# Counting negative entries on GpSimd and TensorE, and a scratch tile for ScalarE's passes, in a two-layer graph kernel

## The chip, the cores and the metric

The kernel runs on one core of a Trainium2 chip. The metric is device time in microseconds (us), the median of three runs.

## The reference

The inputs are `x` (2708 x 512), a sparse non-negative adjacency matrix `adj` (2708 x 2708) and small weights, all float32. Two layers are computed:

```
rowsum = adj.sum(axis=1);  d = where(rowsum > 0, rowsum ** -0.5, 0)
x = layernorm(x + relu((d[:, None] * adj * d[None, :]) @ x @ W + b))
# layer 1: mean over 4 heads of softmax(logits + NEG * (1 - adj)) @ feats, then relu
x = layernorm(x + layer_1(x, adj, W_node, b_node, K))
```

With `NEG` = -1e10, the softmax of a row picks the row's largest entry. The kernel uses that each row of `adj` holds only a few entries. It is exact only where no entry is negative and some other conditions hold, so it keeps a tile `bad` of alarms. If any alarm is set at the end, a dense version (`dense_layers`) runs instead. With the inputs given it does not run.

## The kernel before

**The reading stage.** `adj` is read in 22 blocks of 128 rows (the last has 20 rows), 1.39 MB each, into nine slots. A loop over i = 0 to 21 does, in the order of the program, for each i:

1. load x block i+2 and `adj` block i+1 (SyncE's DMA queue, in this order; `load_blocks`). Block n goes into the slot of block n-9, and is issued once that block is searched (`scanned`) and nobody uses the slot any more.
2. `diagonal(i+1)` on GpSimd (L311): it sets the diagonal of the block to zero and waits for the block's load.
3. `turn(i+1)`: four transposes of x block i+1 on TensorE (L224), copied by ScalarE (L226); then `times(i)`: x block i times `W` on TensorE (L235).
4. `sum_rows(i)`: one pass of ScalarE over block i, written in place, which sums the rows (L299).
5. `root(i)`: five small operations of GpSimd that turn the row sums into `dinv` (L266 to L271).
6. `value(i-1)`: ScalarE scales the product (L540), and the result is stored to `v_d` by a DMA that GpSimd issues (L103); the last three go through SyncE.
7. at i = 3, 7, 10 and 13, `m_load`: weights are loaded, the last three times by an accumulating DMA that GpSimd issues (L491).
8. at i = 10 to 13 `turn_weight` (L497); at i = 14 `b_columns` (L521, L522); at i = 20 `bias_1`: four products on TensorE (L513) and a copy by ScalarE (L515); at i = 21 `pieces(c_3)` on VectorE (L250 to L256), which uses that copy.
9. two searches on VectorE (`find`: MAX8, L318, and FIND_INDEX8, L319), each for a third of a block. After the last third of a block, `under_0` follows on ScalarE (L305): a pass in place that sums the negative parts of the block into `bad`. The searches stay behind the loads: at i two thirds of a block are searched, while a whole block is loaded.
10. at i = 11 `group(0)` and at i = 20 the same for blocks 4 to 11, in the parts `pack_1`, `pack_2` and `pack_3`: VectorE prepares lists; between `pack_1` and `pack_3` lies a small product on TensorE (L334), whose result `pack_3` reads (L369). At i = 13 to 16 the lists of blocks 0 and 1 are made (`hot`, `enlist`, `listed`).

**The order is written by hand** (`tc.manual_schedule()`): each engine runs its instructions in the order in which the program gives them, and waits on semaphores. What is ahead in an engine's queue holds up what is behind it.

**The gathering stage.** After the loop, VectorE goes on with six searches and then with the remaining ones between the chunks of the first layer. Rows of `v_d` are gathered by indirect DMAs that GpSimd issues (L611) and summed on TensorE (L672) and VectorE. When the last search is done, the lists of the remaining blocks are made and the second layer begins. At which point of the program each search stands is fixed.

Numbers of blocks and thirds below count from 0; "third (11, 2)" is the last third of block 11.

Of the kernel before, what the change touches and what calls it, by code (L numbers as in the profile page):

```python
# [63 lines left out]
def tile_two_graph_layers(  # L64
# [65 lines left out]
    sums = const.tile([P, NB], F32, name="sums")  # L130
# [9 lines left out]
    bad = const.tile([P, 2 * NB + 3], F32, name="bad")  # L140
# [9 lines left out]
    bad_i = const.tile([1, 1], I32, name="bad_i")  # L150
# [19 lines left out]
    every = const.tile([P, P], BF16, name="every")  # L170
# [39 lines left out]
    p_one = main.enter_context(tc.tile_pool(name="p_one", bufs=1, space=bass.MemoryType.PSUM))  # L210

    hE = main.enter_context(tc.tile_pool(name="hE", bufs=1))
    NE = 8
    h_early = hE.tile([P, NE, D], F32, name="h_early")
    read = ExitStack()
    SLOTS = 9
    apool = read.enter_context(tc.tile_pool(name="apool", bufs=1))


# [53 lines left out]
    blocks_a = {}  # L273
# [21 lines left out]

    def sum_rows(ib):
        pr = rows(ib)
        a = blocks_a[ib][:pr]
        nc.scalar.activation(a, a, AF.Copy, accum_out=sums[:pr, ib : ib + 1])  # L299

    def under_0(ib):

        pr = rows(ib)
        a = blocks_a[ib][:pr]
        nc.scalar.activation(a, a, AF.Relu, scale=-1.0, accum_out=bad[:pr, NB + ib : NB + ib + 1])  # L305

    def diagonal(ib):

# [243 lines left out]
    for i in range(NB):  # L552
        pr = rows(i)
        if feed:
            load_x(feed.pop(0))
        if i + 1 < NB:
            search_for(i + 1)
            diagonal(i + 1)
            xT[i + 1] = turn(xs.pop(i + 1), rows(i + 1), nc.scalar.copy)
        pos_w[i] = times(xT.pop(i), pr, w_sb, po=p_acc.tile([P, D], F32, name="acc"))  # L560
        sum_rows(i)
        root(dinv[:pr, i : i + 1], sums[:pr, i : i + 1], aii[:pr, i : i + 1])
        if i:
            value(i - 1)
        if i in M_AT:
            m_load(M_AT.index(i))
        if 10 <= i < 10 + ND:
            turn_weight(i - 10)
        elif i == 14:
            b_columns()  # L570
        elif i == NB - 2:
            c_row = bias_1()
        elif i == NB - 1:
            pieces(c_3, c_row)
        if i == NB - 2:
            pack_1(GROUPS[1], GROUPS[2])
        for _ in range(0 if i == NB - 1 else 2 if i else 1):
            if finds[0][0] <= i:
                search_next()
        if i == 11:  # L580
            group(0)
        elif i in (13, 14):
            hot(i - 13)
        elif i in (15, 16):
            enlist(i - 15)
            listed(i - 15)
        elif i == NB - 2:
            pack_2(GROUPS[1], GROUPS[2])
            pack_3(GROUPS[1], GROUPS[2])
# [556 lines left out]
    for ib in range(NS):  # L1146
        pr = rows(ib)
        for c in range(C):
            n = ib * C + c
            form_until(n + 11)  # L1150
            fetch_until(n + (9 if n < 14 else 11) + (0 if found_at is None else min(11, max(0, 2 * (ib - found_at - 3)))))
            add_chunk(ib, c)
            group_of = max(g for g in GROUPS if g <= hot_next)
            if (
                c in (0, 5)
                and hot_next < NS
                and hot_next <= ib + (2 if c == 0 else 4)
                and group_of in starts
                and not (c == 5 and found_at is not None and ib == found_at + 1)
            ):  # L1160
                hot(hot_next)
                listing[n + 4] = lambda k=hot_next: enlist(k)
                listing[n + 6] = lambda k=hot_next: listed(k)
                hot_next += 1
            if n in listing:
                listing.pop(n)()
            if ib == 0 and c in (5, 8):
                weights(2 if c == 5 else 3)
            if finds and c in ((1, 4, 7) if ib < 3 else (1, 5)):
                search_next()  # L1170
            if c == 2 and not finds and found_at is None:
                group(GROUPS[2])
                searching[0] = False
                found_at = ib
            if found_at is not None:
                for f in plan.pop((ib - found_at, c), []):
                    f()
            if c == 2 and ib > ROOTS_AT:
                root_1(ib - 1, ib)
            if c == (2 if ib <= ROOTS_AT else 3) and ib:  # L1180
                k = slice(ib - 1, ib)
                if ib <= ROOTS_AT:
                    norm_2(ib - 1, ib, rows(ib - 1))
                else:
                    root_2(ib - 1, ib)
                    nc.scalar.activation(nbs[:, k], nms[:, k], AF.Copy, scale=rss[:, k])
                norm_3(ib - 1, rows(ib - 1), space(ib - 1))
                store(h_d, space(ib - 1), ib - 1)
                waiting_h.append(ib - 1)
            if c == (7 if ib < EARLY else 6):  # L1190
                for _ in range(2):
                    if waiting_h:
                        turn_h(waiting_h.pop(0))
            for k in sorted(products_u):
                u_store(k)
            if c == (5 if ib < EARLY else 8 if ib == EARLY else 1) or (ib == EARLY and c == 5):
                for k in sorted(hTs):
                    u_product(k)
            if found_at == ib - 3 and c == 4:
                products_l = list(range(NB))  # L1200
            if c % 2 and products_l:
                listed_turn(products_l.pop(0))
            elif len(dl.get("turned", [])) > (2 if products_l else 0):
                listed_product(dl["turned"].pop(0))
            if dl.get("at") == n - 2:
                root_1(L, L + 1)
                root_2(L, L + 1)
                norm_v(L, P, h_of[L])
# [85 lines left out]
    for n in first:  # L1294
        rows_out(n)
    root_2(second[0], second[-1] + 1)
    nc.vector.tensor_copy(bad_i, po[:1, :1])
    for n in second:
        y_3(n)
        rows_out(n)  # L1300
# [146 lines left out]
```

## Time and profile before

| | |
|---|---|
| median of 3 runs | 490.27 us (490.2 to 490.66) |
| the profiled execution's own time | 488.01 us |
| its span (first to last instruction) | 486.3 us |
| busy: TensorE, VectorE, ScalarE, GpSimd | 376.8, 391.7, 312.3, 305.3 us |
| mean granted clock of TensorE | 0.914 |
| `sum_rows`, 22 passes (L299) | 54.8 us |
| `under_0`, 22 passes (L305) | 54.4 us |
| searches, 66 thirds (L318, L319) | 71.7 and 72.1 us |
| `adj` loads: bytes, median time from issue to landing | 21 of 1354 KB, 9.3 us |

Times on the profile count from the start of the span. A line of the timeline gives start, duration, engine, line of the kernel, operation, output and input, number of instructions, and in brackets how long the engine stood idle before and what released it. PE is TensorE, DVE VectorE, ACT ScalarE, POOL GpSimd, SPq SyncE's issue of DMAs. In a line of windows, each engine has its busy time and its instructions; then come TensorE's granted clock, the DMA engines' mean share and the GB/s.

### The profile page before, as it was taken

The page shows a single profiled execution, that of the slowest core. Times are in us where ns is not written, and L with a number is a line of the kernel's source. Part 1 is how long each engine was busy: PE and PEld are TensorE (multiplying, and loading weights), DVE is VectorE, ACT ScalarE, POOL GpSimd, SP SyncE. Part 2 cuts the span into 40 slices and gives each one's busy share as a digit, 9 for nine tenths or more (in the row PEclk, how much of TensorE's full clock was granted, in tenths as well). Part 3 has the DMA queues.
Part 4 walks back from the last instruction along what each step waited for, and adds up shares of the span by engine and source line. Part 5 has one row for each costly group of instructions (what it writes and reads, how often), then busy time and mean ns, then how long its engine had stood idle before and what let it go on. Part 6 is the DMA issues. An engine that isn't in the chain of part 4 may idle for free.

```text
span 486.3 us, 5318 instructions
## 1 busy us (share of the span) xinstructions
PE 376.8 (77%) x1129; PEld 168.8 (35%) x1129; DVE 391.7 (81%) x1079; ACT 312.3 (64%) x575; POOL 305.3 (63%) x434
## 2 busy tenths in 40 slices
PE   4979788788978987799977958699999999880000
PEld 3434344333223333344323423344444444340000
DVE  2799989879799999999999996666667697667661
ACT  1599999797886556776773453865666322348680
POOL 2343544454477677777787577777777665677703
PEclk9998998798997999999999889799999999995555
DMA  7999999998548678889889789999999688469952
GB/s 232 419 398 416 422 339 371 357 336 342 197 119 286 202 235 264 263 253 315 272 258 290 228 261 371 376 325 376 369 367 313 219 270 269 138 194 308 322 193 84
DMA packets 51565, 140.67 MB, mean 289 GB/s; under 512 B 10617, under 2 KB 10617, under 8 KB 48688
## 3 DMA queue, kind: packets, MB, share of 16 engines
q0 software_dynamic: 21840, 68.29, 45.1%
q1 hardware_dynamic: 29684, 71.95, 39.4%
q8 instruction: 11, 0.18, 0.2%
q14 instruction: 30, 0.25, 0.2%
HBM read 117.33 MB, written 24.99 MB: 293 GB/s over the span
## 4 chain that ended last, share of the span: by engine, by line
DVE 28%; PE 19%; DMA 7%; issue 5%; ACT 3%; POOL 3%; POOLq 0%; DVEq 0%; ACTq 0%
PE acc L672 7%; PE po L235 6%; PE acc_l L1012 4%; DVE ats L319 4%; DVE vals L318 3%; DVE hot L393 3%; DVE vs L662 2%; DMA l_a<-in_adj_dram,to_read 2%; DMA g<-u_e,idx 2%; POOL g L611 1%; DVE past L392 1%; DVE h_early L712 1%; DMA g<-v_d,l_col 1%; DVE h_late L1063 1%; DVE vs L711 1%
## 5 line engine op out<-in xcount | busy, mean ns | idle before, releaser
L611 POOL DMA_INDIRECT g<-v_d,l_col x126 | 127.3, 1010 | 42.6 <-issue 22.1
L672 PE MATMUL acc<-g,s 128*128 128x512 f32 x278 | 143.2, 628 | 4.3 <-DMA g<-v_d,l_col 2.6
L235 PE MATMUL acc<-w_sb,sT 128*128 128x512 f32 (+1 forms) x176 | 89.1, 654 | 0.0
L235 PE MATMUL po<-m_sb,sT 128*128 128x512 f32 x176 | 80.8, 603 | 2.7 <-ACT sT L226 2.7
L611 POOL DMA_INDIRECT g<-v_d,cols x63 | 63.4, 1007 | 19.7 <-issue 13.1
L318 DVE MAX8 vals<-a 128x8 f32<-128x896 f32 (+2 forms) x66 | 71.7, 1087 | 2.8 <-ACT a L299 2.8
L319 DVE FIND_INDEX8 ats<-vals,a 128x8 uint32<-128x896 f32 (+2 forms) x66 | 72.1, 1092 | 0.0
L672 PEld LDWEIGHTS acc<-g,s 128*128 128x128 f32 x278 | 49.1, 196 | 50.1 <-issue 42.3
L305 ACT ACTIVATE a<-a 128x2708 f32<-128x2708 f32 (+1 forms) x22 | 54.4, 2471 | 12.4 <-DVE ats L319 12.4
L299 ACT ACTIVATE a<-a 128x2708 f32<-128x2708 f32 (+1 forms) x22 | 54.8, 2490 | 10.0 <-POOL a L311 10.0
L235 PEld LDWEIGHTS po<-m_sb,sT 128*128 128x128 f32 x176 | 33.5, 194 | 45.0 <-issue 38.2
L235 PEld LDWEIGHTS acc<-w_sb,sT 128*128 128x128 f32 (+1 forms) x176 | 34.7, 208 | 38.6 <-issue 38.5
L649 ACT ACTIVATE s<-s,l_val,l_minus 128x128 f32<-128x128 f32 x86 | 42.4, 493 | 2.9
L311 POOL TENSOR_SCALAR_AFFINE_SELECT a<-a 128x128 f32<-128x128 f32 (+1 forms) x22 | 7.2, 327 | 56.0 <-DMA a<-in_adj_dram 49.7
L226 ACT COPY sT<-tp 128x512 f32<-128x512 f32 (+1 forms) x44 | 25.8, 586 | 24.8 <-PE tp L224 24.8
L662 DVE SCALAR_TENSOR_TENSOR vs<-g,scaled,vs 128x512 f32<-128x512 f32 x50 | 37.2, 744 | 0.1
L224 PE MATMUL tp<-ident,x 128*128 128x128 f32 (+1 forms) x88 | 15.4, 303 | 23.6 <-DMA x<-in_x_dram 15.5
L648 ACT ACTIVATE s<-place,l_row 128x128 f32<-128x128 f32 x86 | 33.4, 388 | 0.0
L393 DVE SCALAR_TENSOR_TENSOR hot<-slots,ends,past 128x256 bf16<-128x256 bf16 x63 | 30.6, 485 | 2.2
L1052 POOL DMA_INDIRECT g<-u_e,idx x21 | 21.9, 1041 | 7.1 <-issue 5.5
L726 ACT ACTIVATE nms<-tot 128x1 f32<-128x1 f32 x10 | 2.0, 202 | 34.8 <-DVE h_early L712 19.5
L721 ACT ACTIVATE xr<-h_late,nms 128x512 f32<-128x512 f32 x11 | 7.9, 722 | 24.7 <-DVE nms L720 24.7
(265 smaller groups left out, 579.5 us busy)
## 6 DMA issues: line engine op xcount, KB each, us to landing
a<-in_adj_dram SPq DMA_DIRECT2D x21, 1354.0 KB, 9.3
x<-in_x_dram SPq DMA_DIRECT2D x21, 256.0 KB, 19.1
vs<-v_d SPq DMA_DIRECT2D x21, 256.0 KB, 4.9
xr<-in_x_dram SPq DMA_DIRECT2D x21, 256.0 KB, 5.9
l_v<-v_d SPq DMA_DIRECT2D x21, 256.0 KB, 5.0
u_e<-ut SPq DMA_DIRECT2D x17, 256.0 KB
h_d<-h_late SPq DMA_DIRECT2D x13, 256.0 KB, 2.9
out_dram<-h_late SPq DMA_DIRECT2D x13, 256.0 KB, 4.4
```

The costliest lines, as they stand in the source:

```text
L226: copy(sT[:, :, :pr], ps[:, :, :pr])
L235: nc.tensor.matmul(po[:pr], sT[:, f, :pr], wt[:, f, :], start=(f == 0 and row_3 is None), stop=(f == ND - 1))
L299: nc.scalar.activation(a, a, AF.Copy, accum_out=sums[:pr, ib : ib + 1])
L305: nc.scalar.activation(a, a, AF.Relu, scale=-1.0, accum_out=bad[:pr, NB + ib : NB + ib + 1])
L318: nc.vector.max(out=vals[:pr, ib, t, :], in_=part)
L319: nc.vector.max_index(out=ats[:pr, ib, t, :], in_max=vals[:pr, ib, t, :], in_values=part)
L393: nc.vector.scalar_tensor_tensor(h_t[:, t, :], slots, ends[:, 0, ib - lo, t : t + 1], past, op0=ALU.is_gt, op1=ALU.subtract)
L611: nc.gpsimd.indirect_dma_start(out=t[:pr], out_offset=None, in_=src, in_offset=bass.IndirectOffsetOnAxis(ap=ap, axis=0))
L648: nc.scalar.activation(s[:, :pr], place[:, :pr], AF.Abs, bias=minus_row[:, t : t + 1])
L649: nc.scalar.activation(s[:, :pr], s[:, :pr], AF.Relu, scale=minus_val[:, t : t + 1], bias=val[:, t : t + 1])
L662: nc.vector.scalar_tensor_tensor(vs, g, scaled[:, ib, CHUNKS[c][1], 0:1], vs, op0=ALU.mult, op1=ALU.add)
L672: nc.tensor.matmul(acc[ib][:pr], ss.pop((ib, c))[:k, :pr], g[:k], start=(first and not bias_on_pe(ib)), stop=(c == len(CHUNKS) - 1),)
```

## The change

`sum_rows` and `under_0` write to a new tile `unread` (128 x 2708, bf16) that nobody reads, instead of back into the block.

Seven blocks (1, 3, 5, ... 13, `BY_POOL`) have no `under_0` any more. In its place `below_0(k)` on GpSimd compares a third of such a block with 0 and writes 1 or 0 to a bf16 tile `signs` (two buffers). It stands at i = k + 1, for k = 0 to 19, after `value` and `m_load`: so at i = 18 it takes third (11, 2), at i = 19 and 20 thirds (13, 0) and (13, 1). Of the seven blocks' 21 thirds the loop reaches 20; the last third of block 13 is not compared.

`count_signs` on TensorE sums the tile of the round before with two products of ones by 512 and 384 (or 404) columns into a PSUM tile. It stands just ahead of `below_0`, behind `times(i)`, and ahead of `turn_weight`, `bias_1` and `pack_1` of the same i. In the gathering stage `signs_sum` on ScalarE adds up the counts into `bad`. At the end the alarm sum is compared with 0 instead of being cast.

```
     def sum_rows(ib):
         pr = rows(ib)
-        a = blocks_a[ib][:pr]
-        nc.scalar.activation(a, a, AF.Copy, accum_out=sums[:pr, ib : ib + 1])
+        nc.scalar.activation(
+            unread[:pr], blocks_a[ib][:pr], AF.Copy, accum_out=sums[:pr, ib : ib + 1]
+        )

     def under_0(ib):
         pr = rows(ib)
-        a = blocks_a[ib][:pr]
-        nc.scalar.activation(a, a, AF.Relu, scale=-1.0, accum_out=bad[:pr, NB + ib : NB + ib + 1])
+        if ib in BY_POOL:
+            return
+        nc.scalar.activation(
+            unread[:pr], blocks_a[ib][:pr], AF.Relu, scale=-1.0, accum_out=bad[:pr, NB + ib : NB + ib + 1]
+        )
+    def below_0(k):
+        ib, t = BY_POOL[k // T], k % T
+        w = CUT[t + 1] - CUT[t]
+        s = hE.tile([P, N - CUT[T - 1]], BF16, name="signs", bufs=2)[:, :w]
+        nc.gpsimd.tensor_scalar(s, blocks_a[ib][:, CUT[t] : CUT[t + 1]], 0.0, None, op0=ALU.is_lt)
+        signs.append(s)
+    def count_signs(last):
...
+        s = signs.pop(0)
+        w = s.shape[1]
+        for lo in range(0, w, D):
+            n = min(D, w - lo)
+            nc.tensor.matmul(counted[0][:, :n], every[:, :1], s[:, lo : lo + n], ...)
+    def signs_sum():
+        at = NB + BY_POOL[0]
+        nc.scalar.activation(unread[:1, :D], counted[0], AF.Copy, accum_out=bad[:1, at : at + 1])
...
         if i in M_AT:
             m_load(M_AT.index(i))
+        if signs:
+            count_signs(i == NB - 1)
+        if 0 < i < NB - 1:
+            below_0(i - 1)
         if 10 <= i < 10 + ND:
             turn_weight(i - 10)
...
+            if ib == 1 and c == 6:
+                signs_sum()
...
-    nc.vector.tensor_copy(bad_i, po[:1, :1])
+    nc.vector.tensor_scalar(bad_i, po[:1, :1], 0.0, None, op0=ALU.is_gt)
```

More of the change, by code (lines that the diff above doesn't have):

```diff
@@ L216, in tile_two_graph_layers @@
     SLOTS = 9
+    BY_POOL = range(1, 14, 2)
+    unread = hE.tile([P, N], BF16, name="unread")
     apool = read.enter_context(tc.tile_pool(name="apool", bufs=1))
@@ L297, in sum_rows @@
         pr = rows(ib)
-        a = blocks_a[ib][:pr]
-        nc.scalar.activation(a, a, AF.Copy, accum_out=sums[:pr, ib : ib + 1])
+        nc.scalar.activation(
+            unread[:pr], blocks_a[ib][:pr], AF.Copy, accum_out=sums[:pr, ib : ib + 1]
+        )
     def under_0(ib):
         pr = rows(ib)
-        a = blocks_a[ib][:pr]
-        nc.scalar.activation(a, a, AF.Relu, scale=-1.0, accum_out=bad[:pr, NB + ib : NB + ib + 1])
+        if ib in BY_POOL:
[3 more added lines that the diff above has]
+        )
+    signs = []
+    def below_0(k):
[4 more added lines that the diff above has]
+        signs.append(s)
+    counted = []
+    def count_signs(last):
+        if not counted:
+            counted.append(p_one.tile([P, D], F32, name="acc_l")[:1])
+        s = signs.pop(0)
+        w = s.shape[1]
+        for lo in range(0, w, D):
+            n = min(D, w - lo)
+            nc.tensor.matmul(
+                counted[0][:, :n],
+                every[:, :1],
+                s[:, lo : lo + n],
+                start=(len(counted) == 1),
+                stop=(last and lo + n == w),
+                skip_group_check=True,
+            )
+            counted.append(None)
+    def signs_sum():
+        at = NB + BY_POOL[0]
+        nc.scalar.activation(unread[:1, :D], counted[0], AF.Copy, accum_out=bad[:1, at : at + 1])
     def diagonal(ib):
```

## The prediction

> **What bounds the kernel now.** I read the page first, then the stage that the change touches, by windows and by the DMA view, then that stage's end as a timeline, then VectorE's waits behind it.
>
> ```profile
> span 486.3 us, 5318 instructions
> 80.00:100.00 20.00, 15.61 (x48) 7.51 (x47) 14.95 (x29) 17.25 (x21) 9.47 (x24) 0.83 1.05 359
> 100.00:120.00 20.00, 16.11 (x50) 7.47 (x49) 19.45 (x40) 16.65 (x18) 8.77 (x29) 0.91 1.03 353
> 120.00:140.00 20.00, 19.32 (x48) 6.51 (x47) 16.74 (x44) 18.31 (x26) 10.82 (x26) 1.00 0.40 137
> ```
>
> In the reading stage VectorE and ScalarE look nearly full, but the DMA share is 1.03 to 1.05: the transfers are the limit. In the DMA view of 100:135 (40 slices of 0.875 us) the stream stops only at 120 us:
>
> ```profile
> DMA  9999999999999999999996720099989655007700
> ```
>
> The trace's packet records say the same: from 34.9 us on each block's first packet follows the last one of the block before, up to block 19 (last packet 120.25). Blocks 10 to 18 were issued up to 15 us before their first packet. Block 20 is the first that comes late: its slot was held by `under_0(11)`.
>
> ```profile
> 119.27 2.45 ACT L305 ACTIVATE a<-a 128x2708 f32<-128x2708 f32 x1
> 120.95 0.29 POOL L311 TENSOR_SCALAR_AFFINE_SELECT a<-a 128x128 f32<-128x128 f32 x1 [2.39 <-DVE m L328]
> 121.87 6.62 SPq L99 DMA_DIRECT2D a<-in_adj_dram  x3
> 123.19 0.64 POOL L103 DMA_DIRECT2D v_d<-xr  x1 [0.28 <-issue]
> 126.31 3.60 PE L513 MATMUL po<-h_early,b_e 128*3 128x512 f32 x8
> 128.25 0.29 POOL L311 TENSOR_SCALAR_AFFINE_SELECT a<-a 128x128 f32<-128x128 f32 x1 [4.42 <-DMA a<-in_adj_dram]
> 130.07 0.18 DVE L369 COPY ends<-po 128x24 f32<-128x24 f32 x1 [2.02 <-PE po L334]
> 130.50 0.65 POOL L103 DMA_DIRECT2D v_d<-vs  x1 [0.28 <-issue]
> 131.60 0.56 ACT L515 COPY row<-po 3x512 f32<-3x512 f32 x1
> 132.19 0.42 DVE L250 CAST piece<-row 3x512 bf16<-3x512 f32 x1 [0.61 <-ACT row L515]
> ```
>
> This is the end of the reading stage: `diagonal(19)` at 120.95, the load of block 20 at 121.87, `diagonal(20)` at 128.25. TensorE is ahead of GpSimd here: `bias_1` (L513) runs before `diagonal(20)`. Behind it VectorE resumes at 132.19. From there it never waits again while the searches last:
>
> ```profile
> DVE ends L369 <- PE po L334: 2.0, 1, 2.0
> DVE piece L250 <- ACT row L515: 0.6, 1, 0.6
> ```
>
> These are all of VectorE's waits in 130:260. So the moment at which VectorE gets through L369 and L250 sets the end of the last search, at about 250, and all behind it: a microsecond there is one at the end.
>
> **The change, part by part.** ScalarE loses six passes before 128 us (blocks 1 to 11) and one later (block 13): 7 x 2.65 us (L305 with its read-out) = 18.5 us. I count nothing for them: until 120 us the DMA stream sets the pace, and the one at 141.8 is followed by ScalarE waiting for VectorE. Without that cover they would be a gain.
>
> Writing to a scratch tile frees the first search from `sum_rows(0)`: VectorE's 2.8 us wait for L299, its only one there. The search then runs ahead of loads that are bound by DMA: nothing. `signs_sum` is one short pass on ScalarE (512 columns, as L515, 0.56 us) where VectorE leads; the compare in place of the cast is one operation for one: nothing.
>
> *The price of a compare.* The trace has no wide GpSimd comparison. The nearest rows: GpSimd's narrow comparison (L268) takes 0.23, and its 128-column L311 takes 0.29 where narrow L271 takes 0.19, so about 0.79 ns a column; 895 more columns give 0.23 + 0.70 = 0.93 us (an estimate). From below it is 0.23, that of a narrow one. From above, L268 stretched to 0.76 at 132.93, while VectorE ran L250 and L252: 3.3 times, 3.1 us. I take 0.93, since L311 kept its 0.29 us beside searches (at 109.38, for one).
>
> The Trainium skill's "GPSIMD Engine Reference" (section 3.1) puts a good one-input loop at about 1.8 cycles per element of 1.2 GHz: 1.34 us for 896 elements, 1.57 with the narrow operation; by that the sum would be 1.3 us higher, as two compares lie on the path. The same page calls GpSimd the wrong choice for elementwise work, which speaks against this change.
>
> *The place of a compare.* This decides. Compare and what it holds up, at each round i: GpSimd's queue has `diagonal(i+1)`, `root(i)`, the store of `value(i-1)`, then the compare. So it starts only when block i+1 has landed. At i = 18 it takes third (11, 2), which holds block 20's slot:
>
> - before: block 20 issued at 121.87, when `under_0(11)` was done.
> - after: `diagonal(19)` 120.95; the store behind it ends at 123.83 (2.88 later); compare 0.05 + 0.93; issue at about 124.9. That is 3.0 late. VectorE's search of the third (done at 114.0 before) has 10 us of slack.
> - load to diagonal as before: 128.25 - 121.87 = 6.38, so `diagonal(20)` at 131.3.
>
> That wait also stands on TensorE. At i = 20 its queue has `times(20)`, then `count_signs` of third (13, 0), then `bias_1`, `pack_1`. That third is compared at i = 19, behind `diagonal(20)`:
>
> - store of `value(18)` ends 2.90 after `diagonal(20)` (128.25 to 131.15): 134.2; compare: 135.15.
> - two count products: 0.4 (L513's products of as many columns are 0.43 apart).
> - `bias_1` and `pack_1`: from L513's start to L369's is 3.76 (126.31 to 130.07): 139.3 at full clock.
> - clock: TensorE stands idle some 4 us ahead of that. After a wait of 2.85 us the same eight products took 6.16 instead of 3.60:
>
> ```profile
> 86.18 3.60 PE L235 MATMUL acc<-w_sb,sT 128*128 128x512 f32 x8
> 92.63 1.08 PE L224 MATMUL tp<-ident,x 128*128 128x128 f32 x4 [2.85 <-DMA x<-in_x_dram]
> 93.51 6.16 PE L235 MATMUL acc<-w_sb,sT 128*128 128x512 f32 x8
> ```
>
>   Another such wait (112.0) gave 5.29. I take 1.7 (5.29 - 3.60), from 0 to 2.6: L369 at 141.0.
> - rest of `pack_3`, 130.07 to 131.6: 1.5, so VectorE starts L250 at 142.5. The copy L515 is ready by 141.4.
>
> The sum: 142.5 - 132.19 = 10.3 us. On the profiled execution's 488.01 us (486.3 of span, 1.7 around it) this is 498.3; that execution is 2.26 below the median of the runs, 490.27, to which I add the same 10.3: 500.6, forecast 500.5. The ends: 0.23 per compare and no clock loss give 10.3 - 1.4 - 1.7 = 7.2 (497.5); 3.1 per compare and 2.6 for the clock give 10.3 + 4.3 + 0.9 = 15.5 (505.8).
>
> "TensorE: Matmul & The Clock Gate" in the skill (Part 1) says that a window of about 3.4 us without work halves the clock; the trace shows it after 2.85 us. By the page the loss is certain, and the 497.5 would be 499.2.
>
> *Other places, counted at nothing.* The 40 count products (0.2 us each) lie in TensorE's waits. Their own wait holds up the transposes of the next round, hence ScalarE's `sum_rows`; blocks come every 6.5 us or so from 62 us on, and `diagonal` to count takes about 4, so it fits. At i = 10 the K load is queued ahead of the compare (issued at 76.39, 1.35 us), so `pack_1` of `group(0)` comes at about 79.8 instead of 71.6, and VectorE stands 8 us longer; the stop of 4.7 us at L414 goes in return, and third (11, 2) is searched at about 117, still before 124.8. With that cover gone, block 20 would come later by what is over. At i = 14 `b_columns` moves behind a compare: `diagonal(16)` 0.9 later, block 18 issued at 107.3 instead of 102.93, about when the stream needs it (first packet 107.77): 0 to 1.6.
>
> **The rivals.**
>
> *Faster: the slots come free earlier.* If the compare of third (11, 2) ended ahead of block 19's landing, block 20 could be issued by 119.3 and the gap of 2.6 us in the stream (120.25 to 122.83) would close. VectorE would then resume at about 130.3, set by `bias_1` (block 21 of x arrives behind `adj` block 19): 1.9 gained, 488.4. For it: ScalarE's pass was what block 20 waited for. Against it: `diagonal(19)` is ahead of the compare in GpSimd's queue. It decides if compares run before 118.4.
>
> *Smaller loss: only block 20 is late.* If the count products at i = 20 had their data early, `bias_1` would stay where it is, and L515, behind `sum_rows(20)`, would move by the 3.0 alone: 493.3. Against it: the count stands ahead of `bias_1`.
>
> *No change.* The change drops 18.5 us of ScalarE and adds some 19 us of GpSimd, neither of which bounds the stage; if the tail absorbs the waits the time stays at 490.3. Against it: VectorE's two waits above, which have no slack. The change does not quite do what it says (20 of 21 thirds), which moves nothing here.
>
> **How the numbers follow.** Forecast 0.78 (its own range 497.5 to 505.8); only block 20 late 0.08; faster 0.07; no change 0.04; worse than 507, from compares slowed everywhere, 0.03. A measurement here tells about 0.2% (1 us) from no change. So faster 0.07, same 0.04, slower 0.89. The range leaves out the faster and the unchanged case and takes in the smaller loss: 493 to 507.
>
> **What would show it.** In the profile after: a gap of some 5.6 us in the adj stream ahead of block 20; its issue right behind a GpSimd compare, near 125; `bias_1` behind a GpSimd release near 135; VectorE's wait for the `pack_1` product some 9 us long instead of 2.0; searches starting near 147 instead of 137.07. I am wrong if VectorE resumes before 135, or if block 20 is issued before 122.

## The result and the profile after

The change makes the kernel slower: 507.2 us (median of 4 runs, 506.3 to 510.34) against 490.47 us before (4 runs), a ratio of 1.0337 (95% interval 1.0289 to 1.0384). Measured again later (experiment e12) the ratio was 1.0379 (1.0331 to 1.0427). The forecast was 500.5, with a range of 493 to 507. The direction was right, and so was the chain of waits that makes the loss, but the loss was 16.7 us instead of 10.3: the median lies 0.2 us above the upper end of that range, and e12's 1.3 us above it. Some executions took over 1.5% more than the fastest of their kernel (one of e7 2180 us, one of e8 673); the medians below are over all executions, the ratios over the others, and the profiles of e4, e5 and e8 are of such slower ones.

The profiled execution of the changed kernel took 510.34 us, its span is 508.5. Its windows (columns as in the table's note above):

```profile
80.00:100.00 20.00, 16.54 (x55) 8.28 (x55) 16.00 (x26) 15.65 (x18) 16.58 (x26) 0.91 1.05 360
100.00:120.00 20.00, 14.54 (x52) 6.58 (x52) 19.41 (x40) 14.40 (x17) 17.75 (x33) 0.91 0.82 247
120.00:140.00 20.00, 14.71 (x45) 6.10 (x44) 19.62 (x38) 9.89 (x11) 9.63 (x17) 1.00 0.57 206
140.00:160.00 20.00, 13.94 (x30) 3.83 (x30) 8.27 (x26) 10.86 (x19) 12.47 (x21) 0.74 0.10 39
```

GpSimd (the fifth busy time) went from 9.47 and 8.77 us of 20 to 16.58 and 17.75. The DMA share in 100:120 fell from 1.03 to 0.82: the stream of blocks now waits for GpSimd. The DMA view of 100:145 (40 slices of 1.125 us) shows where:

```profile
DMA  9999999994060479989999820006009999200007
```

In this stretch there are two gaps ahead of `adj` blocks where there was one: ahead of block 18 (no packet of `adj` from 107.4 to 115.6 us) and ahead of block 20 (126.8 to 133.8). The timeline of the first gap, GpSimd and SyncE's queue:

```profile
96.98 1.34 POOL L532 DMA_DIRECT2D h_early<-in_L_gnn_K_dram  x1 [1.22 <-DMA h_early<-in_L_gnn_K_dram]
...
97.82 3.02 POOL L320 TENSOR_SCALAR signs<-a 128x896 bf16<-128x896 f32 x1
...
100.24 0.84 POOL L352 TENSOR_SCALAR_AFFINE_SELECT a<-a 128x128 f32<-128x128 f32 x1
...
103.96 2.49 POOL L320 TENSOR_SCALAR signs<-a 128x896 bf16<-128x896 f32 x1
...
109.19 0.29 POOL L352 TENSOR_SCALAR_AFFINE_SELECT a<-a 128x128 f32<-128x128 f32 x1
...
112.12 2.54 POOL L320 TENSOR_SCALAR signs<-a 128x916 bf16<-128x916 f32 x1
...
114.69 0.33 SPq L99 DMA_DIRECT2D a<-in_adj_dram  x1
```

L320 is the compare, L352 the `diagonal`, L532 a K load. The compare at 112.12 is third (9, 2), whose slot block 18 takes: SyncE issues the load 0.03 us after it ends. The rounds of GpSimd follow each other here without a wait for a landing. The end of the stage:

```profile
127.34 0.29 POOL L352 TENSOR_SCALAR_AFFINE_SELECT a<-a 128x128 f32<-128x128 f32 x1 [1.00 <-DMA a<-in_adj_dram]
...
130.26 2.54 POOL L320 TENSOR_SCALAR signs<-a 128x916 bf16<-128x916 f32 x1
...
132.82 1.73 SPq L99 DMA_DIRECT2D a<-in_adj_dram  x3
...
140.56 0.29 POOL L352 TENSOR_SCALAR_AFFINE_SELECT a<-a 128x128 f32<-128x128 f32 x1 [7.77 <-DMA a<-in_adj_dram]
...
143.53 2.48 POOL L320 TENSOR_SCALAR signs<-a 128x896 bf16<-128x896 f32 x1
...
146.06 0.91 PE L333 MATMUL acc_l<-signs,every 128*1 128x512 bf16 x2 [8.69 <-POOL signs L320]
...
146.76 5.34 PE L554 MATMUL po<-h_early,b_e 128*3 128x512 f32 x8
...
152.26 0.18 DVE L410 COPY ends<-po 128x24 f32<-128x24 f32 x1 [11.24 <-PE po L375]
...
153.69 0.41 DVE L252 CAST piece<-row 3x512 bf16<-3x512 f32 x1
```

L333 is a count, L554 `bias_1`, L410 the read of `pack_3` (L369 before). The chain runs as forecast from `diagonal(19)` (127.34, before 120.95) on: the compare of third (11, 2) ends, block 20 is issued (132.82, before 121.87), `diagonal(20)` follows (140.56, before 128.25), the compare behind it holds the count, the count holds `bias_1`, and VectorE waits. It takes up L252 (L250 before) at 153.69 instead of 132.19, 21.5 us later. This moment is called the *resume* below. VectorE's waits in 130:280 are then

```profile
DVE ends L410 <- PE po L375: 11.2, 1, 11.2
```

and nothing else. The last search starts at 267.9 us instead of 246.3 (L359, before L318), 21.6 later: the shift passes through in full, as forecast.

### The profile page after: what moved, and what is told of

Its sections match the earlier page's. It is cut to its first block, busy times and chain, and to the rows that moved or that the text cites. A ratio compares the mean times of both kernels' runs of the same rounds, so it can differ in the third digit from the quotient of the medians.

```text
span 508.5 us, 5394 instructions
## 1 busy us (share of the span) xinstructions
PE 390.6 (77%) x1169; PEld 172.0 (34%) x1169; DVE 401.3 (79%) x1079; ACT 297.3 (58%) x563; POOL 355.8 (70%) x454
## 4 chain that ended last, share of the span: by engine, by line
DVE 22%; PE 19%; DMA 9%; issue 6%; POOL 3%; ACT 3%; POOLq 1%; DVEq 0%
PE acc L717 8%; PE po L237 6%; PE acc_l L1057 4%; DVE ats L360 4%; DMA g<-u_e,idx 3%; DVE vals L359 3%; DVE hot L434 3%; DVE vs L707 2%; DMA l_a<-in_adj_dram,to_read 2%; DMA g<-v_d,l_col 2%; POOL g L656 1%; DMA u_d<-ut,own_d 1%; DVE past L433 1%; DVE h_early L757 1%; DVE s L698 1%
## 5 line engine op out<-in xcount | busy, mean ns | idle before, releaser
L237 PE MATMUL po<-m_sb,sT 128*128 128x512 f32 x176 | 85.0, 629 | 4.2 <-ACT sT L228 4.2
L237 PE MATMUL acc<-w_sb,sT 128*128 128x512 f32 (+1 forms) x176 | 83.4, 619 | 0.0
L359 DVE MAX8 vals<-a 128x8 f32<-128x896 f32 (+2 forms) x66 | 71.7, 1086 | 0.0
L300 ACT ACTIVATE unread<-a 128x2708 bf16<-128x2708 f32 (+1 forms) x22 | 54.2, 2464 | 11.2 <-POOL a L352 11.1
L320 POOL TENSOR_SCALAR signs<-a 128x896 bf16<-128x896 f32 (+1 forms) x20 | 51.7, 2583 | 0.5
L237 PEld LDWEIGHTS po<-m_sb,sT 128*128 128x128 f32 x176 | 35.1, 203 | 49.7 <-issue 42.0
L237 PEld LDWEIGHTS acc<-w_sb,sT 128*128 128x128 f32 (+1 forms) x176 | 32.9, 198 | 34.7 <-issue 34.6
L333 PE MATMUL acc_l<-signs,every 128*1 128x512 bf16 (+2 forms) x40 | 11.7, 377 | 33.7 <-POOL signs L320 33.7
L309 ACT ACTIVATE unread<-a 128x2708 bf16<-128x2708 f32 (+1 forms) x15 | 36.7, 2449 | 0.0
L434 DVE SCALAR_TENSOR_TENSOR hot<-slots,ends,past 128x256 bf16<-128x256 bf16 x63 | 32.6, 517 | 2.2
L352 POOL TENSOR_SCALAR_AFFINE_SELECT a<-a 128x128 f32<-128x128 f32 (+1 forms) x22 | 8.2, 374 | 28.5 <-DMA a<-in_adj_dram 28.5
L756 DVE TENSOR_TENSOR vs<-acc,vs 128x512 f32<-128x512 f32 x20 | 13.7, 687 | 12.4 <-PE acc L717 12.3
## 6 DMA issues: line engine op xcount, KB each, us to landing
a<-in_adj_dram SPq DMA_DIRECT2D x21, 1354.0 KB, 10.3
```

What stands on the lines that cost most here:

```text
L237: nc.tensor.matmul(po[:pr], sT[:, f, :pr], wt[:, f, :], start=(f == 0 and row_3 is None), stop=(f == ND - 1))
L300: nc.scalar.activation(unread[:pr], blocks_a[ib][:pr], AF.Copy, accum_out=sums[:pr, ib : ib + 1])
L309: nc.scalar.activation(unread[:pr], blocks_a[ib][:pr], AF.Relu, scale=-1.0, accum_out=bad[:pr, NB + ib : NB + ib + 1])
L320: nc.gpsimd.tensor_scalar(s, blocks_a[ib][:, CUT[t] : CUT[t + 1]], 0.0, None, op0=ALU.is_lt)
L359: nc.vector.max(out=vals[:pr, ib, t, :], in_=part)
L434: nc.vector.scalar_tensor_tensor(h_t[:, t, :], slots, ends[:, 0, ib - lo, t : t + 1], past, op0=ALU.is_gt, op1=ALU.subtract)
```

## The experiments

Twelve kernels ran. "The first theory" below is the one that an expectation names first. e1 to e8 ran on another chip than e9 to e12. There the gathering stage takes longer: the kernel before has 532 to 535 us, and from the last search's start to the end the kernel e1 takes 279.0 us (529.8 - 250.8), e11 on the second chip 241.7 (488.0 - 246.3). The reading stage is the same on both, as far as e1, which stands for the kernel before on the first chip, tells (it resumes at 132.12, before at 132.19). So each ratio is against the kernel before on the same chip, and the resume, read from the profile, is the finer measure.

| kernel | median us | before there | ratio (95%) | resume us |
|---|---|---|---|---|
| e1 scratch tile only | 531.8 | 532.02 | 1.0034 (0.998 to 1.0089) | 132.12 |
| e2 seven blocks not sought | 527.84 | 532.02 | 0.995 (0.9896 to 1.0004) | 131.04 |
| e3 compares of 288 columns | 539.91 | 532.02 | 1.0207 (1.009 to 1.0323) | 144.87 |
| e4 compare ahead of `diagonal` | 534.87 | 532.02 | 1.009 (1.0039 to 1.0141) | 137.15 |
| e5 last count behind `bias_1` | 546.26 | 534.74 | 1.0187 (1.0112 to 1.0263) | 147.81 |
| e6 compares, no counts | 541.14 | 534.74 | 1.0158 (1.0088 to 1.0227) | 141.23 |
| e7 only blocks 1, 3, 5, 7 | 539.5 | 534.74 | 1.0084 (1.0031 to 1.0137) | 140.76 |
| e8 only block 11, rounds 11, 12, 14 | 534.84 | 534.74 | 0.9948 (0.9894 to 1.0002) | 136.59 |
| e9 five forms of GpSimd's work | 493.87 (one run) | 490.03 | | 137.49 |
| e10 as e4, no counts | 491.77 | 490.03 | 1.0033 (1.0 to 1.0065) | 135.41 |
| e11 only block 11, rounds 12, 15, 16 | 489.26 | 490.03 | 0.9973 (0.9942 to 1.0003) | 132.10 |
| e12 the changed kernel again | 508.34 | 490.03 | 1.0379 (1.0331 to 1.0427) | 153.59 |

### e1 and e2: the scratch tile, and ScalarE's passes

e1 keeps the scratch tile and gives all blocks back to ScalarE; e2 leaves out the search for negative entries of the seven blocks altogether. Their edits of the changed kernel (e2 has the last three removals only):

```
-    BY_POOL = range(1, 14, 2)
+    BY_POOL = ()
...
-        if signs:
-            count_signs(i == NB - 1)
-        if 0 < i < NB - 1:
-            below_0(i - 1)
...
-            if ib == 1 and c == 6:
-                signs_sum()
```

e1, expected: 

> Part of the change alone: ScalarE's passes write to the scratch tile, all 22 under_0 stay on ScalarE, no compares, no counts. Theory A (the loss comes from where the compares stand in GpSimd's queue, and from the counts behind them in TensorE's): the time of before, 490.3 us within 1; the first search starts some 2.8 us earlier and this brings nothing. Rival D (the scratch tile costs or gains by itself, through another write pattern or new waits between ScalarE's passes): more than 1 us off, either way.

e2, expected: 

> The change without compares and counts: seven blocks are searched for negatives by nobody (that part of the work is left out). Theory A: the adj loads pace the reading stage, so the 18.5 us less on ScalarE bring only the gap ahead of block 20: about 1.9 us, 488.4, between 487 and 490. Rival S (ScalarE was the bound of the stage): well over 5 us gained, 485 or less.

e1 stands where before stood: block 20 issued at 121.82, resume 132.12. Its first search starts at 14.6 instead of 17.1 us, and nothing comes of it. In e2 the gap ahead of block 20 is closed (first packet 119.0) and the resume is 1.1 us earlier; the ratio's interval still holds 1. So the two gains that the change could have had are worth 0 and about 1 us.

### e3: the forecast's own price

```
-        w = CUT[t + 1] - CUT[t]
+        w = CUT[t + 1] - CUT[t] if k == 0 else 288
...
-        nc.gpsimd.tensor_scalar(s, blocks_a[ib][:, CUT[t] : CUT[t + 1]], ...)
+        nc.gpsimd.tensor_scalar(s, blocks_a[ib][:, CUT[t] : CUT[t] + w], ...)
```

All compares but the first look at 288 columns only, which brings their price to about the 0.93 us that the forecast took. Expected: 

> The change with each compare (but the first) cut to the first 288 columns of its third; the rest of those thirds is not searched. At the 2.5 us per 896 columns that the profile after shows, 288 columns take about 0.9 us, which is the price that the prediction assumed; everything else stays where it is. Theory A: the prediction's own sum, 10.3 us over before, 500.6 (498 to 503); block 18 issued by 108 with no gap in the stream, block 20 near 125, the count ahead of bias_1 near 135. Rival B (what costs is GpSimd's load, 52 us of compares, or its contention with VectorE): with 19 us of compares in place of 52, most of the 17 us loss is gone, 494 or less.

```profile
124.59 0.96 POOL L320 TENSOR_SCALAR signs<-a 128x288 bf16<-128x288 f32 x1
...
125.58 2.84 SPq L99 DMA_DIRECT2D a<-in_adj_dram  x3
...
132.66 0.29 POOL L352 TENSOR_SCALAR_AFFINE_SELECT a<-a 128x128 f32<-128x128 f32 x1 [7.10 <-DMA a<-in_adj_dram]
...
136.83 6.45 PE L554 MATMUL po<-h_early,b_e 128*3 128x512 f32 x8
...
144.87 0.41 DVE L252 CAST piece<-row 3x512 bf16<-3x512 f32 x1
```

At 0.96 us a compare the chain of the forecast comes out nearly as summed: block 20 at 125.58 (forecast 124.9), `diagonal(20)` 132.66 (131.3), resume 144.87 (142.5). That is 12.7 us late instead of 10.3. Block 18, however, is issued at 108.78, and 2.3 us of gap stand ahead of it (108.5 to 110.8), where 108 and no gap were expected. What is left to the changed kernel's 21.5, 8.8 us, comes with the compare's true price. (Two smaller differences lie in it: e3's count is one short product instead of two, some 0.5 us less, and its `bias_1` took 6.45 instead of 5.34.)

### e4 and e10: the compare ahead of the diagonal

```
         if feed:
             load_x(feed.pop(0))
+        if 0 < i < NB - 1:
+            below_0(i - 1)
...
-        if signs:
-            count_signs(i == NB - 1)
-        if 0 < i < NB - 1:
-            below_0(i - 1)
+        if len(signs) > 1 or (signs and i >= NB - 2):
+            count_signs(i == NB - 1 and len(signs) == 1)
+        if i == NB - 1 and signs:
+            count_signs(True)
```

In e4 the compare of each round goes ahead of `diagonal(i+1)`, so that it does not wait for a landing. Expected: 

> The same compares at their full width, but each one round i stands ahead of diagonal(i+1) instead of behind the store of value(i-1), so that GpSimd does it while it would wait for the block's load. Counts stay at their place. Theory A: the slots of blocks 18 and 20 come free in time, the counts' data too, and the loss is gone: 488 to 492. Rival C (2.5 us of compare in every round is too much for GpSimd wherever it stands: about 5.6 us of GpSimd work per round against rounds of about 5.6 us): still 497 or more.

e10 is e4 without the counts (the four lines with a + at the end are gone, and so is `signs_sum`: nothing is counted). Expected: 

> Compares ahead of the diagonal as in e4, and no count products and sum (the counting of seven blocks is left out). e4 resumed at 137.15 us, 5.0 later than the kernel with the scratch tile alone. Theory A (these 5 us are GpSimd's round, which the compare lengthens to 5.1 to 5.5 us): resume stays at 135 to 138 us, ratio 1.003 to 1.012. Rival B (they are the count products, for which TensorE and behind it ScalarE and GpSimd wait): resume at 131 to 133.5 us, ratio 0.993 to 1.002.

e4 resumes at 137.15: with the same 20 compares and the same counts, place alone takes away 16.5 of the 21.5 us. The ratios agree: 1.009 against the changed kernel's 1.0379. That leaves 5.0, more than the first theory had for it, and its ratio of 1.009 is above what that theory allows. e10 tells where they lie: without counts it resumes at 135.41, only 1.7 earlier. Its compares stand 5.1 to 5.5 us apart, back to back with GpSimd's other work:

```profile
110.36 2.49 POOL L320 TENSOR_SCALAR signs<-a 128x896 bf16<-128x896 f32 x1
...
115.73 2.48 POOL L320 TENSOR_SCALAR signs<-a 128x896 bf16<-128x896 f32 x1
...
120.83 2.53 POOL L320 TENSOR_SCALAR signs<-a 128x916 bf16<-128x916 f32 x1
...
123.39 0.35 SPq L99 DMA_DIRECT2D a<-in_adj_dram  x1
...
132.57 2.48 POOL L320 TENSOR_SCALAR signs<-a 128x896 bf16<-128x896 f32 x1
...
135.41 0.41 DVE L252 CAST piece<-row 3x512 bf16<-3x512 f32 x1
```

Block 20's load still follows a compare (123.39, before 121.87). So some 3 us come with the compares alone, even at this place, and some 2 with the counts. Not all of the 3 us is GpSimd's lateness: L410 runs at 132.29, 2.3 later than in e1 (130.01), and the rest is VectorE's own. The compare at 132.57 runs beside the short operations between L410 and L252, which take 3.1 us instead of the changed kernel's 1.4. The last section has more of this.

### e5 and e6: the counts

e5 moves the count of round 20 behind `bias_1` and `pack_1`:

```
-        if signs:
+        if signs and i != NB - 2:
             count_signs(i == NB - 1)
...
             pack_1(GROUPS[1], GROUPS[2])
+            count_signs(False)
```

Expected: 

> The changed kernel, but in round 20 the count products stand behind the bias products and the carry product of the search instead of ahead of them. Theory A (of the 21.5 us by which VectorE resumes later, the 8 to 9 us between diagonal(20) and the bias products come from the count in front of them): blocks 18 and 20 are still issued late (about 114.7 and 132.8 us), but the bias products run on the last K load and no longer wait for the compare of round 19; VectorE resumes (its first copy of c_3) near 144.5 us instead of 153.7, that is +12 over the kernel before, ratio near 1.023. Rival (the products cost nothing where they stand, the blocks' lateness alone does it): VectorE resumes at 151 us or later and the ratio stays at 1.034 or above.

e6 leaves all counts out (nothing is counted), with the removals of e1 for `count_signs` and `signs_sum` only. Expected: 

> The changed kernel with its 20 compares on GpSimd, but nothing counts them: no count products on TensorE and no sum of the counts on ScalarE (the counting of the negative entries of seven blocks is left out). Theory A: as with the products moved, since all that the products cost lies in round 20: resume near 144 us, ratio 1.02 to 1.025; blocks 18 and 20 still late, because GpSimd's compares make them so. Rival B (TensorE's waits for compares in the earlier rounds, 33.7 us in 14 times, delay the turned blocks, and these the roots and the loads): blocks 18 and 20 come back towards 107 and 122 us, resume at 140 us or earlier, ratio under 1.016.

e5 resumes at 147.81, 5.9 us earlier than the changed kernel although its block 20 was issued 1.25 later (134.07), and 3.3 later than the first theory had. `bias_1` no longer waits for the compare behind `diagonal(20)`; but the count of the round before still stands ahead of the transposes and `times(20)`, and TensorE's granted clock was 0.50 there (134.1 to 140.9):

```profile
134.10 0.93 PE L333 MATMUL acc_l<-signs,every 128*1 128x512 bf16 x2 [2.89 <-POOL signs L320]
...
135.50 6.38 PE L237 MATMUL acc<-w_sb,sT 128*128 128x512 f32 x8
...
141.81 3.60 PE L554 MATMUL po<-h_early,b_e 128*3 128x512 f32 x8
...
145.56 0.18 DVE L410 COPY ends<-po 128x24 f32<-128x24 f32 x1 [4.22 <-PE po L375]
```

In e6, with no count at all, L410 runs at 132.88, and the resume (141.23) waits for the copy of c_row, queued on ScalarE behind `sum_rows(20)`:

```profile
129.13 3.60 PE L554 MATMUL po<-h_early,b_e 128*3 128x512 f32 x8
...
137.29 0.29 POOL L352 TENSOR_SCALAR_AFFINE_SELECT a<-a 128x128 f32<-128x128 f32 x1 [7.18 <-DMA a<-in_adj_dram]
...
141.23 1.74 DVE L252 CAST piece<-row 3x512 bf16<-3x512 f32 x1 [6.84 <-ACT row L556]
```

Blocks 18 and 20 are still late (issued at 113.37 and 130.13), as the first theory said, but each by 1.3 to 2.7 us less than with counts. So the counts' waits hold up the earlier rounds a little, too. Both theories of e6 caught half of it: the resume lies between their numbers.

### e7, e8 and e11: fewer compares

e7 compares blocks 1, 3, 5 and 7 only, in rounds 1 to 12:

```
-    BY_POOL = range(1, 14, 2)
+    BY_POOL = range(1, 8, 2)
...
-            count_signs(i == NB - 1)
-        if 0 < i < NB - 1:
+            count_signs(i == T * len(BY_POOL) + 1)
+        if 0 < i <= T * len(BY_POOL):
             below_0(i - 1)
```

Expected: 

> The changed kernel, but only blocks 1, 3, 5 and 7 are sought on GpSimd: 12 compares in rounds 1 to 12, none later; the other blocks are ScalarE's. Theory A (compares cost time only in the rounds whose loads and counts are waited for, 15 to 20): blocks 18 and 20 issued near 107 and 121 us, VectorE resumes at 131 to 133 us, ratio 0.995 to 1.005. Rival C (a compare in any round fills GpSimd's round, and the lag is carried along): block 18 issued after 109 us, resume 136 us or later, ratio above 1.008.

This was a miss, and the rival's numbers hold: blocks 18 and 20 are issued at 109.24 and 125.54, no compare runs after round 12, and still the resume is 8.6 us late. VectorE's only wait on L410 is now the one of `group(0)` in round 11:

```profile
DVE ends L410 <- PE po L375: 14.3, 1, 14.3
```

In round 20, L410 runs at 139.34 without a wait, 5.3 us after `pack_1`'s product began (134.06). VectorE itself is late there, for two reasons. Compare, count and K load stand ahead of `group(0)`'s small product, and VectorE waits 14.3 us for it (4.2 in e1); later waits that e1 has are gone in return. And beside the compares some of VectorE's short operations take longer. From its first search to the resume VectorE runs the same instructions in both kernels: in e1 it is busy for 103.7 us and idle for 13.8, in e7 for 108.4 and 16.9, and e7 starts 0.9 later. So of the 8.6 us 3.0 are waiting, 4.7 longer operations and 0.9 the later start. In the changed kernel the same wait is there (13.8 us), and VectorE is busy for 111.4 us, but neither costs anything, since VectorE waits 11.2 us in round 20 anyhow.

e8 compares block 11 only, whose slot block 20 takes:

```
-    BY_POOL = range(1, 14, 2)
+    BY_POOL = (11,)
+    AT = (11, 12, 14)
...
-            count_signs(i == NB - 1)
-        if 0 < i < NB - 1:
-            below_0(i - 1)
+            count_signs(i == AT[2] + 1)
+        if i in AT:
+            below_0(AT.index(i))
```

Expected: 

> Only block 11, whose slot block 20 takes, is sought on GpSimd: three compares in rounds 10, 11 and 12; the other blocks are ScalarE's, all into the scratch tile. Theory A (the slot of block 20 waits for ScalarE's pass over block 11): block 20 is issued near 119 us instead of 121.9, VectorE resumes near 131.0 us, ratio 0.994 to 1.0. Rival (the pass over block 11 is not what holds the slot, or the compares in rounds 10 to 12 delay the first group's lists): block 20 at 121.8 us or later, ratio 1.0 to 1.01.

The kernel that ran compares in rounds 11, 12 and 14, not in 10 to 12 as the expectation says.

Time and profile do not fit together: the ratio, 0.9948, is that of the first theory, while the profiled run (538.97, above the median) resumes at 136.59 with block 20 issued at 121.35. In it a count stands ahead of the product that `hot` waits for, and VectorE waits 8.95 us for that. It settles nothing about the slot.

e11 takes the counts out of the way: it compares in rounds 12, 15 and 16, behind which GpSimd waits 3.6 to 4 us for a landing in the kernel before, and has all counts in round 18:

```
+    AT = (12, 15, 16)
...
-        if signs:
-            count_signs(i == NB - 1)
-        if 0 < i < NB - 1:
-            below_0(i - 1)
+        if i in AT:
+            below_0(AT.index(i))
+        if i == 18:
+            for k in range(T):
+                count_signs(k == T - 1)
```

with `BY_POOL = (11,)` and three buffers of `signs`. Expected: 

> Only block 11 is sought on GpSimd, in the rounds 12, 15 and 16, in which GpSimd waits 3.5 to 4 us for a landing anyhow, with all its counts in round 18, where no search's carry waits behind them; three tiles for the answers instead of two. Theory (a compare that fits into GpSimd's wait and a count that nobody waits behind cost nothing, and block 11's slot comes free without ScalarE's second pass): block 20 issued at 118.5 to 120.5 us, VectorE resumes at 130.5 to 131.5 us, ratio 0.993 to 1.0. Rival (the compares still push a diagonal or a root): block 20 at 121.8 us or later, resume 132 us or later, ratio 1.0 to 1.01.

```profile
114.64 14.16 SPq L99 DMA_DIRECT2D a<-in_adj_dram  x3
...
117.67 1.30 PE L334 MATMUL acc_l<-signs,every 128*1 128x512 bf16 x6
...
126.92 3.60 PE L555 MATMUL po<-h_early,b_e 128*3 128x512 f32 x8
...
130.67 0.18 DVE L411 COPY ends<-po 128x24 f32<-128x24 f32 x1 [2.79 <-PE po L376]
```

Block 20 is issued at 114.64, right behind the last compare, and its packets follow block 19's at once (first 119.3, last 125.3; before 122.8 and 127.8), as the theory said. Yet VectorE resumes at 132.10, as the rival said and as before, for a reason that neither had: TensorE works without a stop from 117.67, partly on the counts, and `bias_1` starts at 126.92 (before 126.31). The last search starts at 246.3, as before. The 2.5 us that block 20 gained met TensorE as the next bound; e2, with no compares and no counts, resumes only 1.1 us earlier. This valid version is no faster than the kernel before by more than the measurement tells (0.9942 to 1.0003); none that was tried is.

### e9: what GpSimd charges for

```
-        nc.gpsimd.tensor_scalar(s, blocks_a[ib][:, CUT[t] : CUT[t + 1]], 0.0, None, op0=ALU.is_lt)
+        part = blocks_a[ib][:, CUT[t] : CUT[t + 1]]
+        if k % 5 == 0:
+            nc.gpsimd.tensor_scalar(s, part, 0.0, None, op0=ALU.is_lt)
+        elif k % 5 == 1:
+            nc.gpsimd.tensor_copy(s, part)
+        elif k % 5 == 2:
+            nc.gpsimd.tensor_scalar(s[:, :448], part[:, :448], 0.0, None, op0=ALU.is_lt)
+        elif k % 5 == 3:
+            nc.gpsimd.tensor_scalar(s, part, 0.0, None, op0=ALU.max)
+        else: ... the compare of 448 columns into an f32 tile
```

Expected: 

> The changed kernel without count products and sum (the counting is left out), and its 20 GpSimd instructions in five forms by turns: the compare of 896 or 916 columns into bf16; a plain copy of them into bf16; the compare of 448 columns into bf16; the maximum with 0 of 896 or 916 columns into bf16; the compare of 448 columns into f32. Theory A (the price is one of columns, whatever is done with them: 0.97 us at 288 and 2.49 at 896 make 2.5 ns a column and 0.25 us fixed): copy and maximum 2.45 to 2.6 us, both compares of 448 columns 1.3 to 1.4 us. Rival 1 (the compare itself is dear): copy at the affine select's slope, under 1.2 us. Rival 2 (the turn from f32 to bf16 is dear): 448 columns into f32 under 0.8 us.

From the timeline, one of each form (L322 is the compare, L324 the copy, L326 the compare of 448 columns, L328 the maximum, L331 the compare into f32):

```profile
48.91 1.36 POOL L331 TENSOR_SCALAR signs_f<-a 128x448 f32<-128x448 f32 x1
...
82.64 2.49 POOL L322 TENSOR_SCALAR signs<-a 128x896 bf16<-128x896 f32 x1
...
101.21 2.49 POOL L328 TENSOR_SCALAR signs<-a 128x896 bf16<-128x896 f32 x1
...
119.68 0.94 POOL L324 CAST signs<-a 128x896 bf16<-128x896 f32 x1
...
124.81 1.36 POOL L326 TENSOR_SCALAR signs<-a 128x448 bf16<-128x448 f32 x1
```

Compare and maximum cost the same 2.49 us, into bf16 or f32 is the same, and the price goes with the columns: (2.49 - 1.36) / 448 = 2.5 ns a column. But a plain copy of the same 896 columns takes 0.94 us. So the column theory fails at the copy, and the first rival has the copy's time right but not its reason: the maximum is as dear as the comparison. The second rival fails. These two operations with a scalar have a slope of 2.5 ns, the copy one of some 0.8 (an estimate: (0.94 - 0.23) / 895, with the narrow operation's 0.23). A clash with VectorE does not make the price either: the changed kernel's compare at 143.53 took 2.48 while VectorE stood idle (141.0 to 152.3).

### e12: the changed kernel again

Expected: 

> The changed kernel itself beside these runs, so that all parts are compared with it on one chip. Both theories: the reading stage repeats, block 18 issued near 114.7, block 20 near 132.8, VectorE resumes near 153.7 us (21.5 later than before), ratio 1.03 to 1.045; if the end of the kernel is set by something later on this chip, the resume shifts as said and the ratio stays under 1.03.

No edit. Block 18 is issued at 113.86, block 20 at 133.12, the resume is at 153.59 and the last search at 267.9. The ratio is 1.0379. The reading stage repeats within a microsecond, and so does the last search.

## Why the prediction was right, and where its size was off

**What bounds the kernel; ScalarE's 18.5 us at nothing.** Right, nearly. e1 shows the scratch tile at 0, e2 the passes at 1.1 us of resume.

**The price of a compare, 0.93 us: the mis-sized term.** Measured: 2.48 to 2.54, and 3.02 to 3.06 behind a K load. The estimate took the slope of the affine select (0.79 ns a column). By e9 this is about the slope of a copy, not that of a compare or a maximum with a scalar, and the narrow rows, 1 column wide, could not show the difference. The range between its ends, 0.23 and 3.1, did hold the price; the choice inside it was wrong. The sum's two compares on the path cost 2 x 1.57 = 3.1 us more.

The Trainium skill's "GPSIMD Engine Reference" (section 3.1) has 1.03 cycles per element of 1.2 GHz for very short loop bodies and 1.8 for a good unrolled loop. The copy is near the first (0.8 ns is 0.95 such cycles). The compare, at 2.5 ns or 3.0 cycles, is above the second, so the page's price would have been too low as well. Its warning against elementwise work on GpSimd fits the outcome, though no run here has the same compare on VectorE.

**The place of the compare, and `bias_1` behind its count.** Right, link by link: block 20's issue behind the compare, `diagonal(20)`, compare, count, `bias_1`, L410. e4 shows the place at 16.5 of 21.5 us, e5 the count of round 20 at 5.9 or more. These two overlap and do not add up.

**"Block 18 ... about when the stream needs it: 0 to 1.6". This step failed.** It counted one compare ahead of `diagonal(16)`, 0.9 us, and behind it that of third (9, 2). But two stand ahead of it (rounds 13 and 14), GpSimd already comes 1.9 us later to the K load of round 13 (96.98, before 95.08), and in before's trace GpSimd waited only 0.55 and 0.22 us for landings there (at 96.97 and 102.45), so nothing hid the compares. `diagonal(16)` came at 109.19 instead of 102.45, block 18 was issued at 114.69, not 107.3, and the stream stood still until 115.6. So `diagonal(19)`, from which the sum counts, came at 127.34, 6.4 us later than before. Even near the forecast's price block 18 was issued at 108.78, with 2.3 us of gap (e3).

**Load to `diagonal(20)`, 6.38 us.** 7.74 measured, 1.4 more; in e3, e6 and e12 7.1, 7.2 and 7.6. It was carried over from a run in which block 21's load came later.

**The clock.** Right: `bias_1` took 5.34 at a granted clock of 0.50 (140.1 to 150.2), the 1.7 us over 3.60 that the sum had. Its count took 0.91 instead of the 0.54 at full clock, 0.3 more than the sum's 0.4 for both from start to start (0.70). The Trainium skill's "TensorE: Matmul & The Clock Gate" (Part 1) has the half clock after an idle window of about 3.4 us; the wait here was 8.69 us. In e5 the products ran at half clock after a wait of 2.89 us, so there a shorter one was enough, as in the prediction's trace (2.85).

These terms add up: 10.3 + 3.1 + 6.4 + 1.4 + 0.3 = 21.5 us, the shift of the resume.

**The shift passes 1:1 to the end.** Right up to the last search (21.6 us). From profile to profile the span grew by 22.2 (508.5 - 486.3) and 19.9 (506.2 - 486.3, e12), but the medians only by 16.7 and 18.3. Before's profiled execution lay 2.5 us under its median, after's 3.1 over. From the start of the last search to the end the profiles have 240.0 us before, 240.6 and 238.3 with the change (e12), and 241.7 and 241.2 in e11 and e10: a scatter about as large as what is missing. So whether some of the shift is given back behind the last search stays open; no run was made for it. The resume moved by twice the forecast's 10.3 us, and that the medians moved by less and so came nearer to the forecast is luck.

**Counted at nothing.** `group(0)`'s longer stop (13.8 us; the forecast added 8 to at most 2.0) was hidden, as said, but only because round 20's wait came later: e7 shows it uncovered.

**The rivals.** "Faster" needed compares ahead of 118.4. e11 has them and closes the gap, and the time does not move: TensorE holds VectorE where it was, which this rival's 130.3 left out. "Smaller loss" needed an early count at i = 20; e6, without counts, shows that even then the lateness of blocks 18 and 20 costs 9.0 us. "No change" is excluded by the ratio. Neither the sum nor a rival had VectorE's own operations slowed beside a compare (e7, e10).

## What to carry to other kernels

Price an operation by a row of the same operation at a similar width: the slope of a select or a copy was not that of a compare with a scalar here, and a factor of 2.7 in the price became some 8.8 us in the end (e3). An instruction added to a loop lengthens an engine's round, so before a step is called "in time" count every copy of it that stands between the last wait with slack and the event, not only the one next to it. A consumer that waits for an idle-looking engine, put ahead of a short exchange between other engines (here a count ahead of `bias_1`, `group(0)`'s and `hot`'s products), hands that wait on to all of them: put it behind.

## What the runs showed of the hardware that was not expected

- GpSimd, 128 partitions: 0.94 us for a copy of 896 f32 columns into bf16, 2.49 for a compare or a maximum with a scalar (e9).
- GpSimd's instructions right behind a K load that it issues show some 0.55 us more: compare 3.02 instead of 2.49 us, the `diagonal` behind it 0.84 instead of 0.29 (97.82 and 100.24 above). In the kernel before, where `diagonal` came 0.55 us after the K load had ended (96.97), it kept its 0.29.
- Beside a compare on GpSimd, some short operations of VectorE take 0.5 to 1.9 us longer. The first three lines are from the changed kernel, the last is the same operation as the third in the kernel before (L380, L421 after):

```profile
84.38 1.22 DVE L418 TENSOR_SCALAR most<-most 128x4 f32<-128x4 f32 x1
...
84.61 2.49 POOL L320 TENSOR_SCALAR signs<-a 128x896 bf16<-128x896 f32 x1
...
85.71 1.42 DVE L421 TENSOR_SCALAR eighth<-eighth 128x4 f32<-128x4 f32 x1
```

```profile
72.86 0.17 DVE L380 TENSOR_SCALAR eighth<-eighth 128x4 f32<-128x4 f32 x1
```

  Up to 160 us the changed kernel has eight operations of VectorE that took over 0.5 us more than the shortest of their line, all of them beside a compare (one of `hot`'s at 97.17 took 2.42 instead of 0.48); the kernel before and e1 have none. The searches keep their 1.07 to 1.11 us. What the two engines share there, no run shows.
- `diagonal(20)`'s release came 2.5 us after the last packet counted for block 20 (138.1) and 0.2 after block 21's (140.3), where the two loads were issued together; before, with block 21 later, 0.4 us after its own. e3, e5, e9 and e12 show the same (1.9 to 2.5 us after their own). In e6 it came 1.9 us after its own and 0.1 before block 21's last, so block 21 is not shown to be the cause. Whether one of the DMA engines was late with its share of block 20, the trace does not tell.
- The same kernel takes 490 us on one chip and 532 to 535 on another. The difference lies behind the reading stage, whose end agrees within 0.1 us (before against e1). The record does not tell why.
